# Which engine reads the small products of a four-layer network: from VectorE to ScalarE in layers 2 and 3

## The chip, the cores and the metric

The kernel runs on one core of a Trainium2 chip. The core has a matrix engine (TensorE, PE in the profile; its weight loads are PEld), VectorE (DVE), ScalarE (ACT), GpSimd (POOL) and SyncE (SP), which issues transfers. Each engine works through its own list of instructions, and semaphores tie the lists together. Matmul results land in a small accumulator memory, PSUM, and another engine has to read them out of it; in this kernel VectorE and ScalarE do that.

The metric is the time on the device in microseconds (us), the median of several executions. Before the change it is 2778.64 us, the median of 3 executions that lie between 2772.06 and 2782.84.

## What is computed

The input `x` is 4 images of 512 channels and 32x32 pixels (1024 tokens), in float32. Four layers follow one another. Each normalizes by groups (32 groups of 16 channels), computes something, and adds it to its input:

```python
x = x + L0(gn(x))   # attention, 8 heads, heads mixed before the softmax, instance norm of the probabilities
x = x + L1(gn(x))   # channel gate: mean over pixels -> 9-qubit circuit -> linear -> sigmoid, times gn(x)
x = x + L2(gn(x))   # attention, 8 heads, 1x1 convolutions for q, k, v and output
x = x + L3(gn(x))   # memory: the 8 best of 2048 items per token, softmax, weighted sum

def gn(v, G=32, eps=1e-5):
    g = v.reshape(B, G, C // G, H, W)
    m = mean(g, axis=(2, 3, 4)); s = var(g, axis=(2, 3, 4))
    return (g - m) / sqrt(s + eps)
```

Besides the large products there are thus many tiny ones. For each group norm the means and the deviations of 512 channels are averaged over groups of 16 channels, by a matmul with a constant 128x128 matrix. The gate of layer 1 needs two small matmuls for the circuit, one for its nine expectation values and one for the linear layer. Each of these yields at most 128x4 numbers.

## The kernel before

The kernel handles layers 0 and 1 image by image in a first loop and layers 2 and 3 in later loops. Work of the next or the last image that has to be fitted in between is written as Python generators: each `yield` ends a step, and the main loop takes a step or two between its large pieces. `pin` keeps an instruction in program order on its engine.

The group norm of all layers:

```python
def group_coeffs_parts(mean, var, tag):
    ...
    ps = small_ps(f"gps_{tag}")
    pin(nc.tensor.matmul(ps[:, 0:n], gavg, mean, start=True, stop=True))
    gm = tile_("gm")
    pin(nc.vector.tensor_copy(gm, ps[:, 0:n]))
    yield
    dm, sq = tile_("dm"), tile_("gsq")
    nc.gpsimd.tensor_sub(dm, mean, gm)
    nc.gpsimd.tensor_mul(sq, dm, dm)
    nc.gpsimd.tensor_add(sq, sq, var)
    yield
    ps2 = small_ps(f"gps2_{tag}")
    pin(nc.tensor.matmul(ps2[:, 0:n], gavg, sq, start=True, stop=True))
    ve = tile_("gve")
    pin(nc.vector.tensor_scalar_add(ve, ps2[:, 0:n], GN_EPS))
    yield
    rstd = tile_("grstd")
    rsqrt(rstd, ve)                      # on GpSimd
    yield gm, rstd, dm
```

The gate of layer 1 uses it with the tag `b`, layer 2 with `c`, layer 3 with `d`. After it the gate's generator, `gating(b)`, goes on in the same manner:

```python
    # twice, for the two layers of the circuit:
    ps = small_ps(f"amp_{b}_{l}"); products(ps)
    u = small.tile([P, KC], F32, tag="amp", ...)
    pin(nc.vector.tensor_copy(u, ps[:, 0:KC]))
    yield
    ...                                  # the last two qubits are rotated on GpSimd
    # expectation values
    ps = small_ps(f"z_{b}"); ...         # 8 matmuls of one column
    pin(nc.vector.tensor_copy(zr, ps[0:NQ, 0:2]))
    pin(nc.vector.reciprocal(zr[:, 1:2], zr[:, 1:2]))
    yield
    nc.gpsimd.tensor_mul(zr[:, 0:1], zr[:, 0:1], zr[:, 1:2])
    yield
    ps = small_ps(f"gate_{b}"); ...      # 4 matmuls of one column
    pin(nc.vector.tensor_copy(gate, ps[:, 0:KC]))
    yield
    nc.gpsimd.tensor_add(gate, gate, fcb)
    yield
    pin(nc.scalar.activation(gate, gate, AF.Exp, scale=-1.0))
    ...
```

At the border between layer 1 and layer 2 the PSUM pools are set up anew. From there a small product takes a buffer of the pool that holds the attention scores, which has three:

```python
stage.close()
pairs.clear()
stage = ctx.enter_context(ExitStack())
ps_s = stage.enter_context(tc.tile_pool(name="ps_s2", bufs=3, space=PSUM))
ps_m = stage.enter_context(tc.tile_pool(name="ps_m2", bufs=2, space=PSUM))

def small_ps(name):
    return ps_s.tile([P, 2 * NB], F32, tag="sc", name=name)
```

The main loop of layer 2 works in units. A unit is four blocks of 128 keys for two heads and 512 queries; 16 units make an image. While the scores of a unit are made, the values of the unit before it are summed:

```python
def scores2(b, u, before=None):
    def exp2():
        e = places2[:, count[0] % 6]; count[0] += 1
        nc.scalar.activation(e, scs[len(es)], AF.Exp); es.append(e)
    for i, t in enumerate(range(t0, t0 + 4)):
        sc = ps_s.tile([P, 2, NB], F32, tag="sc", ...)
        for r in range(2):
            pin(nc.tensor.matmul(sc[:, r, :], k block, q block, start=True, stop=True))
        scs.append(sc)
        if before is None or i < 2:
            exp2()
    if before is not None:
        apply2(b, before, exp2)          # 8 matmuls into pv; the last two exp2() in between
    ...                                  # sums of the exponentials: gpsimd.tensor_add, vector.tensor_add

def finish2(b):                          # every second unit, at the head of apply2
    rsp = ps_s.tile([P, 2, NB], F32, tag="sc", ...)[:, 0, :]
    ...                                  # two matmuls with ones: the row sums
    nc.scalar.copy(ri, rsp)
    nc.vector.reciprocal(ri, ri)
    nc.vector.tensor_mul(o, pv, ri)
    ...                                  # two gpsimd.dma_start of a row of ri

for b in range(B):
    behind = ...                         # norm3(b - 1), tag d; for b = 0 the gating of the last images
    ahead = ...                          # prepare2(b + 1), tag c
    for s, u in enumerate(UNITS2):
        ...
        if s >= 1: scores2(b, u, UNITS2[s - 1])
        for _ in range(2):
            if s >= 3: next(behind, None)
            if s >= 8: next(ahead, None)
```

So the small steps of `behind` and `ahead` stand between one unit and the scores of the next. (A float32 matmul shows as two in the profile, so the 8 of a unit's scores are 16 there.)

Of the kernel before, what the change touches and what calls it, by code (L numbers as in the profile page):

```python
# [20 lines left out]
KC = C // P  # L21
# [6 lines left out]
NQ = 9  # L28
# [4 lines left out]
GN_EPS = 1e-5  # L33
# [8 lines left out]
def fast_net(ctx: ExitStack, tc: tile.TileContext, a: dict, out: bass.AP, flag: bass.AP):  # L42
    nc = tc.nc
# [12 lines left out]
    def pin(ins):  # L56

        return tc.keep_in_program_order(ins)

    def small_ps(name):  # L60
        return pt_bank
# [60 lines left out]
    def rsqrt(dst, src):  # L122

        nc.gpsimd.tensor_tensor(
            dst, src, mhalf[:dst.shape[0], :dst.shape[1]], ALU.pow
        )


    def group_coeffs_parts(mean, var, tag):

        n = mean.shape[1]

        def tile_(name):
            return small.tile(
                [P, n], F32, tag=f"{name}{n}{tag[0]}", bufs=2, name=f"{name}_{tag}")

        ps = small_ps(f"gps_{tag}")
        pin(nc.tensor.matmul(ps[:, 0:n], gavg, mean, start=True, stop=True))  # L140
        gm = tile_("gm")
        pin(nc.vector.tensor_copy(gm, ps[:, 0:n]))
        yield
        dm, sq = tile_("dm"), tile_("gsq")
        nc.gpsimd.tensor_sub(dm, mean, gm)
# [3 lines that stand above are left out]
        ps2 = small_ps(f"gps2_{tag}")  # L149
        pin(nc.tensor.matmul(ps2[:, 0:n], gavg, sq, start=True, stop=True))  # L150
        ve = tile_("gve")
        pin(nc.vector.tensor_scalar_add(ve, ps2[:, 0:n], GN_EPS))
        yield
        rstd = tile_("grstd")
        rsqrt(rstd, ve)
        yield gm, rstd, dm

    def coeffs(mean, var, tag):

        found = None  # L160
        for found in group_coeffs_parts(mean, var, tag):
            if found is None:
                yield
        return found
# [109 lines left out]
    def first():  # L274
# [13 lines left out]
        def stats(k):  # L288
            mv = small.tile([P, 2], F32, tag="mv0", name=f"mv0_{k}")
            st = small.tile([P, 2, 6], F32, tag="bnst", name=f"st_a0_{k}")  # L290
            for i in range(2):
                pin(nc.vector.bn_stats(st[:, i, :], xn[:, k, i * NB:(i + 1) * NB]))
            pin(nc.vector.bn_aggr(mv, st.rearrange("p i s -> p (i s)")))
            parts[k] = group_coeffs_parts(mv[:, 0:1], mv[:, 1:2], f"a0_{k}")
# [490 lines left out]
    def gating(b):  # L785

        mv1 = img[b]["mv1"]
        gm, rstd, dm = yield from coeffs(mv1[:, 0, :], mv1[:, 1, :], f"b{b}")
        y = small.tile([P, KC], F32, tag="amp", name=f"amp_{b}")
        nc.gpsimd.tensor_mul(y, dm, rstd)  # L790
        yield

        def turned(l, products):
            ps = small_ps(f"amp_{b}_{l}")
            products(ps)
            u = small.tile([P, KC], F32, tag="amp", name=f"amp_{b}_{l}")
            pin(nc.vector.tensor_copy(u, ps[:, 0:KC]))
            yield
            us = small.tile([P, 2, KC], F32, tag="ampt", name=f"ampt_{b}_{l}")
            for i in range(2):  # L800
                for n in range(2):
                    a_ = sincos[:, n, l * NQ + i:l * NQ + i + 1]
                    nc.gpsimd.tensor_scalar_mul(us[:, n], u, a_)
                u_v, sin_v, cos_v = (t.rearrange("p (hi t lo) -> p hi t lo", t=2, lo=2 >> i)
                                     for t in (u, us[:, 0], us[:, 1]))
                nc.gpsimd.tensor_sub(u_v[:, :, 0], cos_v[:, :, 0], sin_v[:, :, 1])
                nc.gpsimd.tensor_add(u_v[:, :, 1], cos_v[:, :, 1], sin_v[:, :, 0])
            return u

        u = yield from turned(0, lambda ps: pin(nc.tensor.matmul(  # L810
            ps[:, 0:KC], turn[:, 0], y, start=True, stop=True)))
        yield

        def second(ps):
            pin(nc.tensor.matmul(ps[:, 0:KC:2], turn[:, 1], u[:, 0:KC:3], start=True, stop=True))
            pin(nc.tensor.matmul(ps[:, 1:KC:2], turn[:, 2], u[:, 1:3], start=True, stop=True))

        u = yield from turned(1, second)
        pr = small.tile([P, KC], F32, tag="amp", name=f"pr_{b}")
        nc.gpsimd.tensor_mul(pr, u, u)  # L820
        yield
        ps = small_ps(f"z_{b}")
        for i, m in enumerate((signs, None)):
            for k in range(KC):
                pin(nc.tensor.matmul(
                    ps[0:NQ, i:i + 1], ones[:, 0:NQ] if m is None else m[:, k, :],
                    pr[:, k:k + 1], start=(k == 0), stop=(k == KC - 1),
                ))
        zr = small.tile([NQ, 2], F32, tag="zr", name=f"zr_{b}")
        pin(nc.vector.tensor_copy(zr, ps[0:NQ, 0:2]))  # L830
        pin(nc.vector.reciprocal(zr[:, 1:2], zr[:, 1:2]))
        yield
        nc.gpsimd.tensor_mul(zr[:, 0:1], zr[:, 0:1], zr[:, 1:2])
        yield
        ps = small_ps(f"gate_{b}")
        for k in range(KC):
            pin(nc.tensor.matmul(
                ps[:, k:k + 1], fcw[:, k * P:(k + 1) * P], zr[:, 0:1], start=True, stop=True))
        gate = small.tile([P, KC], F32, tag="gate", name=f"gate_{b}")
        pin(nc.vector.tensor_copy(gate, ps[:, 0:KC]))  # L840
        yield
        nc.gpsimd.tensor_add(gate, gate, fcb)
        yield

        pin(nc.scalar.activation(gate, gate, AF.Exp, scale=-1.0))
        yield
        nc.gpsimd.tensor_scalar_add(gate, gate, 1.0)
        yield
        pin(nc.vector.reciprocal(gate, gate))
        yield  # L850
        s1 = const.tile([P, KC], F32, tag=f"s1_{b}", name=f"s1_{b}")
        t1 = const.tile([P, KC], F32, tag=f"t1_{b}", name=f"t1_{b}")
        nc.gpsimd.tensor_mul(s1, rstd, gate)
        nc.gpsimd.tensor_mul(t1, gm, s1)
        nc.gpsimd.tensor_scalar_mul(t1, t1, -1.0)
        nc.gpsimd.tensor_scalar_add(s1, s1, 1.0)
        mv2 = const.tile([P, 2, KC], F32, tag=f"mv2_{b}", name=f"mv2_{b}")
        nc.gpsimd.tensor_mul(mv2[:, 0, :], mv1[:, 0, :], s1)
        nc.gpsimd.tensor_add(mv2[:, 0, :], mv2[:, 0, :], t1)
        nc.gpsimd.tensor_mul(mv2[:, 1, :], mv1[:, 1, :], s1)  # L860
        nc.gpsimd.tensor_mul(mv2[:, 1, :], mv2[:, 1, :], s1)
        l2[b] = (mv2, s1, t1)
# [332 lines left out]
    def mid(b, s):  # L1195
        before = b - 1
        if s == TC - 1:
            state["sum_v"] = sum_v(b)
        if TC - 1 <= s <= TC:
            next(state["sum_v"])  # L1200
        if b > 0:
            if s == 3:
                state["norm"] = instance_norm(before)
            if 3 <= s < 7 or OUT - 2 <= s <= OUT:
                next(state["norm"], None)
            if OUT <= s + 1 < OUT + 16 and s % 2:
                image_piece(before, (s + 1 - OUT) // 4, (s + 1 - OUT) // 2 % 2)
            if OUT < s <= OUT + 16 and s % 2 == 0:
                piece_out(before, (s - 2 - OUT) // 4, (s - 2 - OUT) // 2 % 2)
            if s == NEXT:  # L1210
                state["behind"] = chain(state["behind"], gating(before))
        if NEXT - 3 <= s:
            next(state["ahead"])
        next(state["behind"], None)
# [41 lines left out]

    stage.close()
    pairs.clear()
    stage = ctx.enter_context(ExitStack())
    ps_s = stage.enter_context(tc.tile_pool(name="ps_s2", bufs=3, space=PSUM))  # L1260
    ps_m = stage.enter_context(tc.tile_pool(name="ps_m2", bufs=2, space=PSUM))
# [18 lines left out]
    for b in range(B):  # L1280
        last = b + 1 == B
        behind = chain(
            behind if b else state["behind"], norm3(b - 1) if b > 0 else gating(B - 1))
        ahead = prepare3(0) if last else prepare2(b + 1)
        for s, u in enumerate(UNITS2):
# [697 lines left out]
@with_exitstack  # L1983
def net_kernel(ctx: ExitStack, tc: tile.TileContext, a: dict, out: bass.AP):


    with tc.tile_pool(name="keep", bufs=1) as keep:
        flag = keep.tile([1, 1], mybir.dt.int32, tag="flag", name="flag")
        fast_net(tc, a, out, flag)
        again = tc.nc.values_load(flag, min_val=0, max_val=1)  # L1990
    with tc.If(again > 0):
        general_net(tc, a, out)
# [61 lines left out]
```

## Time and profile before

| | value |
|---|---|
| median of 3 executions | 2778.64 us (2772.06 to 2782.84) |
| span of the profiled execution | 2776.2 us |
| mean granted TensorE clock | 0.982 of full speed |
| first and last score matmul of layer 2 start | 1380.9 and 2250.0 us |
| 1375 to 2260 us: TensorE, VectorE, ScalarE, GpSimd busy | 847.3, 326.9, 304.4, 356.9 of 885 us |
| 2360 to 2460 us (in layer 3): TensorE, VectorE busy | 100.0, 80.5 of 100 us |
| duration of a small read on VectorE (128x4, from PSUM) | 0.15 us |

The page of the profile gives the busy time of each engine over the whole span, the span in 40 slices, and the costliest groups of instructions. Other views of the same trace are used too. The waits list, for each engine, which instruction sat idle until which other one had ended, with the total, the number and the longest. The timeline lists instructions in order of time, with consecutive ones of the same kind merged into a row (start, length, engine, line of the kernel, operation, output and inputs, and in brackets the idle time before it and what ended it). The table by stage gives busy time and granted clock in chosen stretches. In all of them an L with a number is a line of the kernel; the names `gps_`, `gm`, `gve`, `amp`, `z`, `zr` and `gate` are the small products and the tiles they are read into, `sc_c` the scores of layer 2, `pv_c` its sums of values, `rs_c` its row sums, and `eT` and `e` the buffers of its exponentials and their sums.

### The profile page before, as it was taken

How to read it: one execution, taken by the hardware profiler on the slowest of the kernel's cores; microseconds unless marked ns; L12 is line 12 of the kernel's file. 1: busy time of each engine (PE TensorE's matmuls, PEld its weight loads, DVE VectorE, ACT ScalarE, POOL GpSimd, SP SyncE). 2: the span in 40 equal slices, each digit the busy share in tenths (PEclk: the TensorE clock that was granted, in tenths of full speed). 3: DMA queues.
4: the chain of work that ended last, by engine and by line, in shares of the span. 5: the costliest groups of instructions: out<-in, count | busy, mean ns of one | idle time of the engine just before them, and what ended most of it. 6: DMA issues, size and time to landing. Idle time of an engine off the chain costs nothing.

```text
span 2776.2 us, 46960 instructions
## 1 busy us (share of the span) xinstructions
PE 2597.5 (94%) x18286; PEld 1178.0 (42%) x18286; DVE 1502.6 (54%) x2407; ACT 1005.8 (36%) x1128; POOL 1243.1 (45%) x1947
## 2 busy tenths in 40 slices
PE   7988998989989898989989999999999999999995
PEld 3443444545445444545433433343344334444442
DVE  4488347871578426872234224413523446888886
ACT  0466336551565426551144024214512532221210
POOL 2266415552456515553066026304601635666664
PEclk9999999999999999999999999999999999999997
DMA  2488537880687527784400030021002016766665
GB/s 77 107 209 203 139 87 212 219 216 30 165 217 207 157 80 196 194 216 175 142 3 1 31 121 1 16 73 64 1 31 91 1 35 189 217 185 215 184 185 149
DMA packets 159321, 349.82 MB, mean 126 GB/s; under 512 B 32361, under 2 KB 65129, under 8 KB 155378
## 3 DMA queue, kind: packets, MB, share of 16 engines
q1 hardware_dynamic: 86304, 167.04, 20.9%
q0 software_dynamic: 51200, 142.93, 19.1%
q10 hardware_dynamic: 21586, 36.76, 4.5%
q8 instruction: 147, 2.41, 0.4%
q14 instruction: 84, 0.69, 0.1%
HBM read 178.57 MB, written 33.69 MB: 76 GB/s over the span
## 4 chain that ended last, share of the span: by engine, by line
PE 75%; DMA 7%; ACT 6%; POOL 4%; DVE 4%; issue 2%; SPq 1%; ACTq 0%; POOLq 0%; DVEq 0%
PE at L1068 16%; PE sc L425 7%; PE mx L183 7%; PE sc_c L947 6%; PE pv L485 6%; PE pv_c L980 6%; DMA s<-ss 5%; PE pt L384 4%; ACT ss L431 4%; PE sc L183 4%; PE p L183 3%; PE v L195 3%; PE k L183 3%; PE q L183 3%; PE pt L658 3%
## 5 line engine op out<-in xcount | busy, mean ns | idle before, releaser
L458 DVE STREAM_TRANSPOSE eT<-e 128x1024 f32<-128x1024 f32 x256 | 317.4, 1242 | 275.5 <-ACT e L452 273.8
L438 POOL DMA_DIRECT2D s<-ss x512 | 259.7, 515 | 399.2 <-ACT ss L431 327.4
L1085 POOL DMA_INDIRECT got<-in_mem,ix x256 | 277.8, 1085 | 210.1 <-DVE tmx L1091 94.9
L941 ACT ACTIVATE eT<-sc_c 128x1024 f32<-128x1024 f32 x256 | 248.1, 1021 | 316.2 <-PE sc_c L947 232.8
L431 ACT COPY ss<-sc 128x1024 f32<-128x1024 f32 x256 | 258.9, 1011 | 260.3 <-PE sc L425 203.2
L474 DVE BATCH_NORM_STATS2 st<-e 128x6 f32<-128x256 f32 x1024 | 341.6, 405 | 0.0
L965 POOL TENSOR_TENSOR e<-eT 128x1024 f32<-128x1024 f32 x96 | 227.8, 2374 | 208.1 <-ACT eT L941 177.7
L425 PE MATMUL sc<-k,q 64*32 64x512 f32 x4096 | 287.6, 617 | 24.6 <-ACT ss L431 19.5
L452 ACT ACTIVATE e<-mx 128x1024 f32<-128x1024 f32 x256 | 262.5, 1028 | 69.9 <-PE mx L445 29.4
L966 DVE TENSOR_TENSOR eT<-eT,e 128x1024 f32<-128x1024 f32 x96 | 122.5, 1277 | 303.4 <-POOL e L965 303.4
L947 PE MATMUL sc_c<-q,k 64*128 64x512 f32 x1024 | 248.4, 618 | 37.7 <-ACT eT L941 9.8
L485 PE MATMUL pv<-eT,v 128*64 128x128 f32 x4096 | 256.9, 280 | 0.0
L485 PEld LDWEIGHTS pv<-eT,v 128*64 128x64 f32 x4096 | 226.7, 139 | 64.1 <-issue 62.5
L980 PE MATMUL pv_c<-eT,v 128*64 128x512 f32 x1024 | 234.5, 600 | 0.0
L445 PE MATMUL mx<-s,wmix 32*32 32x512 f32 x4096 | 159.4, 618 | 42.4 <-DMA s<-ss 40.6
L1109 DVE SCALAR_TENSOR_TENSOR acc<-got,et,acc 128x512 f32<-128x512 f32 x224 | 168.5, 752 | 8.0
L947 PEld LDWEIGHTS sc_c<-q,k 64*128 64x128 f32 x1024 | 93.2, 189 | 176.5 <-issue 74.6
L1007 DVE RECIPROCAL ri_c<-ri_c 128x512 f32<-128x512 f32 x32 | 107.0, 3345 | 96.1 <-ACT ri_c L1006 96.1
L1073 ACT COPY att<-at 128x1024 f32<-128x1024 f32 x64 | 64.8, 1012 | 217.1 <-PE at L1068 217.0
L961 POOL TENSOR_TENSOR eT<-eT 128x1024 f32<-128x1024 f32 x32 | 75.6, 2361 | 145.1 <-ACT eT L941 144.9
L561 POOL TENSOR_TENSOR o<-pv,rb 64x256 f32<-64x256 f32 x128 | 111.2, 868 | 64.6 <-ACT pv L548 57.6
L980 PEld LDWEIGHTS pv_c<-eT,v 128*64 128x64 f32 x1024 | 70.9, 138 | 156.1 <-issue 155.8
(314 smaller groups left out, 3293.2 us busy)
## 6 DMA issues: line engine op xcount, KB each, us to landing
s<-ss SPq DMA_DIRECT2D x512, 128.0 KB
s<-ss POOLq DMA_DIRECT2D x512, 128.0 KB, 4.5
rb<-r POOLq DMA_DIRECT2D x64, 128.0 KB, 5.8
o<-o SPq DMA_DIRECT2D x32, 256.0 KB
xr<-in_x ACTq DMA_DIRECT2D x32, 256.0 KB
x<-xr SPq DMA_DIRECT2D x32, 256.0 KB
xr_c<-x SPq DMA_DIRECT2D x32, 256.0 KB
x<-xr_c SPq DMA_DIRECT2D x32, 256.0 KB
```

What stands on the lines that cost most here:

```text
L183: pin(nc.tensor.matmul(ps[:, n, :], w[:, k, m * P:(m + 1) * P], rhs(k, n), start=(k == 0), stop=(k == KC - 1),))
L425: pin(nc.tensor.matmul(sc[m * NS:(m + 1) * NS, r, :], q[r * HD:(r + 1) * HD, m, s * NS:(s + 1) * NS], k_[r * HD:(r + 1) * HD, m, n * NB:(n ...
L431: pin(nc.scalar.copy(ss[:, :, n * NB:(n + 1) * NB], sc))
L438: pin(relays[r].dma_start(out=s2[r * KC + m::NH], in_=ss[m * NS:(m + 1) * NS, r, :]))
L452: pin(nc.scalar.activation(e[:, half].rearrange("p r qq k -> p (r qq k)"), flat2(pairs[f"mx{half}"]), AF.Exp))
L458: pin(nc.vector.transpose(eT[:, j % 2].rearrange("p b (qq i r) x -> p i r qq b x", qq=2, i=4)[:, i, 2 * half:2 * half + 2], e[:, half].rea ...
L474: pin(nc.vector.bn_stats(st[:, i, 2 * half + r, qq, :], e[:, half, r, qq, :]))
L485: pin(nc.tensor.matmul(pv[r * HD:(r + 1) * HD, gp, :], I["v"][:, t, g * HD:(g + 1) * HD], eT[:, j % 2, t, :, 4 * g:4 * g + 4], start=(t == ...
L947: pin(nc.tensor.matmul(sc[:, r, :], I["k"][r * HD:(r + 1) * HD, m, t * P:(t + 1) * P], I["q"][r * HD:(r + 1) * HD, m, n * NB:(n + 1) * NB] ...
L980: pin(nc.tensor.matmul(pv[r * HD:(r + 1) * HD, :], I["v"][:, t, h * HD:(h + 1) * HD], e[:, r, :], start=(t == 0), stop=(t == TC - 1),))
L1068: pin(nc.tensor.matmul(sc[:, n * NB:(n + 1) * NB], xn3[b][:, k, tt * P:(tt + 1) * P], memT[k][:, i0:i0 + NB], start=(k == 0), stop=(k == K ...
L1085: pin(nc.gpsimd.indirect_dma_start(out=got[:, i, :], out_offset=None, in_=a["mem"], in_offset=bass.IndirectOffsetOnAxis(ap=ix[:, i:i + 1], ...
```

## The change

From the border between layers 1 and 2 on, the small products are read out of PSUM by ScalarE in place of VectorE. It is meant to let a small product give back its buffer without standing in VectorE's list behind longer instructions. The deviations were read with the constant `GN_EPS` added in the same instruction; now ScalarE copies them, and GpSimd adds the constant in a further one. The reads on ScalarE are not pinned to program order. Layers 0 and 1 keep their reads, except for those gates that are still being worked on when layer 2 begins.

```diff
+    by_scalar = []
+
+    def take_small(dst, ps):
+
+        if by_scalar:
+            nc.scalar.copy(dst, ps)
+        else:
+            pin(nc.vector.tensor_copy(dst, ps))
...
         gm = tile_("gm")
-        pin(nc.vector.tensor_copy(gm, ps[:, 0:n]))
+        take_small(gm, ps[:, 0:n])
         yield
...
         ve = tile_("gve")
-        pin(nc.vector.tensor_scalar_add(ve, ps2[:, 0:n], GN_EPS))
+        if by_scalar:
+            nc.scalar.copy(ve, ps2[:, 0:n])
+            nc.gpsimd.tensor_scalar_add(ve, ve, GN_EPS)
+        else:
+            pin(nc.vector.tensor_scalar_add(ve, ps2[:, 0:n], GN_EPS))
         yield
...
             u = small.tile([P, KC], F32, tag="amp", name=f"amp_{b}_{l}")
-            pin(nc.vector.tensor_copy(u, ps[:, 0:KC]))
+            take_small(u, ps[:, 0:KC])
             yield
...
         zr = small.tile([NQ, 2], F32, tag="zr", name=f"zr_{b}")
-        pin(nc.vector.tensor_copy(zr, ps[0:NQ, 0:2]))
+        take_small(zr, ps[0:NQ, 0:2])
         pin(nc.vector.reciprocal(zr[:, 1:2], zr[:, 1:2]))
...
         gate = small.tile([P, KC], F32, tag="gate", name=f"gate_{b}")
-        pin(nc.vector.tensor_copy(gate, ps[:, 0:KC]))
+        take_small(gate, ps[:, 0:KC])
         yield
...
     stage.close()
     pairs.clear()
+    by_scalar.append(True)
     stage = ctx.enter_context(ExitStack())
```

## The prediction, made before the changed kernel was run

> **What bounds the kernel now.** I read the page first, for which engine fills the span; then who TensorE waits for in the stretch the change touches; then one such wait in the timeline; then the clock.
>
> Busy time and share of the span, from the page:
>
> ```profile
> PE 2597.5 (94%) x18286; PEld 1178.0 (42%) x18286; DVE 1502.6 (54%) x2407; ACT 1005.8 (36%) x1128; POOL 1243.1 (45%) x1947
> ```
>
> TensorE sets the time, and no other engine is over 54%. The change switches on when layer 2's loop begins, and layer 2 runs from 1381 us (first `sc_c` matmul) to about 2260. In 1375 to 2260 the table of busy time by stage gives TensorE 847.3 of 885 us: 37.7 us idle. The waits of TensorE in that window say for whom (waiter, released by: us in total, times, longest):
>
> ```profile
> PE sc_c L947 <- ACT eT L941: 9.8, 4, 4.8
> PE sc_c L947 <- DVE gm_d L142: 5.6, 3, 2.1
> PE sc_c L947 <- DVE amp L797: 4.6, 2, 2.9
> PE sc_c L947 <- DVE gve_c L152: 3.3, 2, 1.6
> PE sc_c L947 <- DVE gve_d L152: 3.1, 3, 1.0
> PE sc_c L947 <- DVE xr L624: 2.3, 1, 2.3
> PE sc_c L947 <- DVE gm_c L142: 2.2, 2, 1.1
> PE sc_c L947 <- DVE zr L830: 2.0, 1, 2.0
> PE sc_c L947 <- DVE gm_b L142: 1.8, 1, 1.8
> PE sc_c L947 <- DVE gate L840: 1.4, 2, 1.0
> PE sc_c L947 <- DVE gve_b L152: 1.0, 1, 1.0
> ```
>
> Without `xr` and `eT`, nine of these lines name a small product that VectorE reads: 5.6+4.6+3.3+3.1+2.2+2.0+1.8+1.4+1.0 = 25.0 us in 17 waits, two thirds of the idle time. All hit `sc_c`, the score tile, because small products and scores share three PSUM buffers: the product takes one, the next two score tiles take the others, and the third score tile needs the product's buffer back. (Where two products follow each other, the second score tile already does.) One wait in the timeline (start, us, engine, line, operation):
>
> ```profile
> 1669.37 3.34 DVE L1007 RECIPROCAL ri_c<-ri_c 128x512 f32<-128x512 f32 x1
> ...
> 1670.54 0.39 PE L140 MATMUL gps_d<-mv_d,gavg 128*128 128x4 f32 x2
> ...
> 1672.76 1.23 DVE L966 TENSOR_TENSOR eT<-eT,e 128x1024 f32<-128x1024 f32 x1
> ...
> 1673.90 0.68 DVE L1008 TENSOR_TENSOR eT<-pv_c,ri_c 128x512 f32<-128x512 f32 x1
> 1674.50 0.15 DVE L142 COPY gm_d<-gps_d 128x4 f32<-128x4 f32 x1
> ...
> 1674.71 1.99 PE L947 MATMUL sc_c<-q,k 64*128 64x512 f32 x8 [1.87 <-DVE gm_d L142]
> ```
>
> The product is finished at 1670.93. Its 0.15 us copy starts at 1674.50, because a 3.34 us reciprocal, an addition and a multiplication stand ahead of it on VectorE. TensorE starts two score tiles, then stands 1.87 us.
>
> The idle time is not the whole cost. An undisturbed set of four score tiles takes 3.63 us until the next operation starts (1689.99 in the chain; also 1705.21 to 1708.85). With `gm_d` it takes 1670.85 to 1676.62, 5.77: 2.14 more for 1.87 idle, since after the stall the two halves no longer overlap end to start (about 0.27 each). Two stalls cost much more, and the clock says why (stretch: us, TensorE busy, granted clock, DMA):
>
> ```profile
> 1466.00:1470.20 4.20, 4.20 (x14) 0.66 0.00 0
> 1478.50:1483.00 4.50, 4.47 (x12) 0.62 0.00 0
> ```
>
> They follow the 2.94 us wait for the second `amp` and the 2.01 us wait for `zr`. Twelve matmuls that should take 2.72 us (12 x 0.227) take 4.18 and 4.47.
>
> [...] the 0.15 us copy sat behind 5.25 us of work. [...] half-clock stretches follow these two stalls, [...] and the 2.12 us wait for the third `gm_d` (2163.13) shows none. [...] `ri_c` copies stand among exponentials with no gap of their own (0.59 us for 512 columns), and the 128x4 activation on `gate` takes 0.21 us.
>
> **The change part by part.** Set side by side, the instruction streams of the two kernels are the same on TensorE and on SyncE; VectorE loses 21 small reads, ScalarE gains 21, GpSimd gains 8 additions of the constant.
>
> 1. Removed from VectorE: 21 x 0.15 = 3.2 us. VectorE is busy 327 of 885 us here; this alone is worth nothing.
> 2. Added to ScalarE: 21 x about 0.21 = 4.4 us, an estimate from the `gate` activation. ScalarE is busy 304 of 885 us. In its order each copy stands after the fourth exponential of one unit and before the first of the next. In the example ScalarE is free from 1670.30 to 1672.09, so the copy would start just after 1670.93 and be done about 1671.2. The third score tile wants the buffer at about 1672.6 (1670.85 + 2 x 0.87). No stall is left. In the double cases the first buffer is wanted 0.87 us after the first score tile starts (1461.90 + 0.87 = 1462.77; the two `amp` products end about 1461.74, copy until about 1462.0): enough too.
> 3. Added to GpSimd: 8 x about 0.23 = 1.8 us (the 128x4 constant addition on `gate` is 0.23). GpSimd is busy 357 of 885 us. The addition lengthens the chain to the next small product, which lies a unit (7.2 us) later, and the chain starts about 3 us earlier. Hidden.
> 4. Taken off TensorE's path. I add, for each of the 17 stalls, the time from the first score tile to what follows the fourth, less 3.63:
>  - last image's gating: `gate` 1.26, `gm_b` 2.08, `gve_b` 1.31, first `amp` 1.93, second `amp` 4.62, `zr` 3.98, second `gate` 0.66: 15.8 us
>  - group norm before layer 3: `gm_d` 2.14, 1.93, 2.39 and `gve_d` 3 x 1.32: 10.4 us
>  - group norm before layer 2: `gm_c` 2 x 1.39, `gve_c` 2 x 1.92: 6.6 us
>
>  Sum 32.9 us: 25.0 idle, 17 x 0.27 = 4.6 of broken overlap, and 3.1 of half clock.
> 5. In layer 3 two reads move, `gm_d` and `gve_d` of the last image. TensorE has no idle stretch there (100.00 of 100 us from 2360 to 2460); the 3.5 and 2.0 us that VectorE waited for these products are slack. Worth 0.
>
> GpSimd's order also improves: the DMA issue that waits for the reciprocal now often stands behind the small chain rather than ahead of it.
>
> I keep 31.5 of 32.9: 2778.6 - 31.5 = 2747.
>
> **The rivals.**
> - *Another wait takes the place.* With the stalls gone, units in the gating stage run at TensorE's 7.2 to 8.1 us, and GpSimd, busy 78 of 135 us in 1375 to 1510, must keep up with rotations and sums. It frees the exponentials' buffers; ScalarE already waited 3.8 us for `amp` and 2.5 us for `e` there. For it: these waits lie exactly in this stage. Against it: 78 + 1 of the 119 us left is 67%, the waits followed late VectorE reads, and the next product of the chain has 2 to 3 us of margin by my count. If true, a third of the 15.8 us goes: 2752.
> - *ScalarE becomes late.* A copy that waits for its product holds up the exponentials behind it. Against it: the product always precedes those scores on TensorE, so the copy never waits longer than they do; and ScalarE is at 34%. If it cost 0.3 us in each of 17 places: 2752.
> - *The wait is a label and the real one is behind it.* The fourth score tile waits for the first exponential anyway. In undisturbed units 16 score matmuls run 3.63 us without a gap, so that wait is met in time. If it hid half of each stall: about 2762.
> - *More than the sum.* Only where fewer idle stretches also change the clock elsewhere (the half-clock stretch after the image start at 1391 follows an untouched wait). At most some 3 us: 2743.
>
> **Range and chances.** The three times before span 2772 to 2783, so the noise is about 5 us. The sum gives 2747, the likely rivals 2752, the worst 2762: I take 2739 to 2760. A gain over 2% would need 55.6 us, more than all the idle time of TensorE in layer 2 (37.7 us): chance 0.01. Slower by over 2% would need a new wait of over 3 us at each of 17 places: 0.01.
>
> **What would show it.** Right: no line of TensorE's waits in layer 2 names a small product; the image-start waits (`eT` 9.8, `xr` 2.3, `xr_c` 0.5) stay; the score stretches after a product take 3.6 us; the clock in the gating stage has no half stretch but the first; the copies on ScalarE take about 0.2 us within 0.5 us of their product; layer 2 is about 32 us shorter, layers 0, 1 and 3 unchanged. Wrong: `sc_c` waiting for ScalarE's `gm`, `gve` or `amp`, or for `eT`, by several us in all; small matmuls waiting for GpSimd; or a half clock that stays.

## The result and the profile after

The changed kernel takes 2751.86 us (median of 6 runs, 2747.59 to 2757.4); the kernel before took 2780.18 us beside it (6 runs). The ratio is 0.9901 (95% interval 0.9884 to 0.9918): 28.3 us less, 1.0%. Predicted were 31.5 us less, 2747.

Layer 2, from its first score product to its last row-sum product, went from 877.6 us (1380.87 to 2258.46 in the trace before) to 853.2 us (1378.20 to 2231.35): 24.4 us less. Layers 0 and 1, which the change does not touch, ended 2.7 us earlier. The start of layer 2 lies between 1373.7 and 1391.7 us in the traces of this study, so those 2.7 us are not put down to the change, and the length of layer 2 is a better gauge than the whole time.

The page of the changed kernel, busy time by engine:

```profile
PE 2588.1 (94%) x18286; PEld 1177.9 (43%) x18286; DVE 1520.4 (55%) x2386; ACT 1007.7 (37%) x1149; POOL 1264.0 (46%) x1955
```

VectorE has 21 instructions fewer, ScalarE 21 more, GpSimd 8 more, as counted. The waits of TensorE from layer 2 to the end (waiter, releaser: us in total, times, longest):

```profile
PE stp L1127 <- DVE acc L1122: 19.9, 2, 12.5
PE sc_c L960 <- ACT eT L954: 10.2, 4, 4.6
PE amp L828 <- POOL amp L820: 4.3, 1, 4.3
PE sc_c L960 <- DVE xr L637: 2.3, 1, 2.3
```

The nine lines that named a small product, 25.0 us in 17 waits, are gone. The image starts (`eT` 10.2, before 9.8) and `xr` are as they were, and so is the `stp` wait at the end of layer 3; the 0.5 us for `xr_c`, which were to stay, are gone too. One line is new: the product of the second half of a rotation waits 4.3 us for GpSimd. TensorE and GpSimd around it, from the timeline (start, us, engine, line, operation, in brackets idle time and releaser):

```profile
1448.89 0.57 POOL L816 TENSOR_SCALAR ampt<-amp,sincos 128x4 f32<-128x4 f32 x2
1454.39 1.10 POOL L1024 DMA_DIRECT2D fcw<-ri_c  x2 [4.93 <-issue]
1455.50 0.21 POOL L819 TENSOR_TENSOR amp<-ampt 128x2 f32<-128x2 f32 x1
1455.65 0.20 POOL L820 TENSOR_TENSOR amp<-ampt 128x2 f32<-128x2 f32 x1
```
```profile
1455.91 0.59 PE L828 MATMUL amp<-amp,turn 128*128 128x2 f32 x2 [4.30 <-POOL amp L820]
...
1457.29 6.14 PE L960 MATMUL sc_c<-q,k 64*128 64x512 f32 x16
```

A pair of row transfers (`fcw<-ri_c`, two rows of reciprocals that the kernel tests for their range at its end) stands on GpSimd between the two products of the second rotation and the two additions that finish it. GpSimd is free at 1449.46 and stands 4.93 us in front of it. TensorE needs the result at about 1451.6 and gets it at 1455.85. In the kernel before, the same pair stood ahead of the whole first rotation:

```profile
1456.71 1.13 POOL L1011 DMA_DIRECT2D fcw<-ri_c  x2 [3.06 <-issue]
1457.86 0.60 POOL L803 TENSOR_SCALAR ampt<-amp,sincos 128x4 f32<-128x4 f32 x2
```

In the changed kernel, after the wait, the score set takes 6.14 us and the small products 0.57 to 0.59 us, both longer than undisturbed (3.70 and 0.36 to 0.39 us). The table by stage shows why (stretch: us, busy of TensorE, weight loads, VectorE, ScalarE, GpSimd, granted clock, DMA share, GB/s):

```profile
1455.90:1463.40 7.50, 7.49 (x24) 3.80 (x24) 1.25 (x1) 2.38 (x4) 7.50 (x12) 0.58 0.00 0
1463.40:1470.00 6.60, 6.60 (x48) 2.75 (x48) 3.53 (x2) 3.01 (x6) 5.54 (x7) 1.00 0.01 2
```

In the slow stretch the score set's weight loads, taken two at a time, start every 0.85 us (1458.31, 1459.16, 1460.01), in the set at 1468.59 every 0.43 us: this is the half clock.

The wait and the half clock after it (score set 2.44 us over 3.63, the small products some 0.6) cost about 7.4 us: the gating stretch, from the first `gate` product to the second score set after the second `gate` product, went from 81.45 to 73.07 us, 8.4 less where 15.8 were to come. In the second image the stretch with both norms (from the score set before `gm_d` to the one after `gve_c`) went from 69.19 to 62.44, 6.75 less for the 6.77 that the prediction has for its four stalls.

### The profile page after: what moved, and what is told of

The parts are those of the page before. It is cut to its first block, busy times and chain, and to the rows that moved or that the text cites. A ratio compares the mean times of both kernels' runs of the same rounds, so it can differ in the third digit from the quotient of the medians.

```text
span 2749.0 us, 46995 instructions
## 1 busy us (share of the span) xinstructions
PE 2588.1 (94%) x18286; PEld 1177.9 (43%) x18286; DVE 1520.4 (55%) x2386; ACT 1007.7 (37%) x1149; POOL 1264.0 (46%) x1955
## 4 chain that ended last, share of the span: by engine, by line
PE 81%; DMA 7%; ACT 5%; DVE 3%; issue 1%; POOL 1%; SPq 1%; ACTq 0%; POOLq 0%; DVEq 0%
PE at L1081 16%; PE sc_c L960 8%; PE pv_c L993 8%; PE sc L438 7%; PE mx L196 7%; PE pv L498 6%; DMA s<-ss 4%; PE pt L397 4%; PE p L196 4%; PE sc L196 4%; ACT ss L444 4%; PE v L208 3%; PE k L196 3%; PE q L196 3%; PE pt L671 3%
## 5 line engine op out<-in xcount | busy, mean ns | idle before, releaser
L979 DVE TENSOR_TENSOR eT<-eT,e 128x1024 f32<-128x1024 f32 x96 | 132.9, 1384 | 276.0 <-POOL e L978 276.0
L960 PE MATMUL sc_c<-q,k 64*128 64x512 f32 x1024 | 244.3, 616 | 12.5 <-ACT eT L954 10.2
```

What stands on the lines that cost most here:

```text
L960: pin(nc.tensor.matmul(sc[:, r, :], I["k"][r * HD:(r + 1) * HD, m, t * P:(t + 1) * P], I["q"][r * HD:(r + 1) * HD, m, n * NB:(n + 1) * NB] ...
```

## The experiments

Every kernel was timed beside the kernel before on its own chip. "Layer 2" is its length in the profiled run, 877.6 before and 853.2 after. "Image starts" are the four waits of a score product for an exponential at the start of an image, and behind the plus sign what the half clock after them cost: a stretch's length times one less its granted clock, for the 7.5 us after each of these waits, and between the first score product and the first of them. Such stretches at the second and third image, first in the changed kernel, then in the one with rows by SyncE (columns as in the table by stage above):

```profile
1646.88:1654.38 7.50, 7.50 (x28) 2.42 (x30) 0.00 (x0) 2.96 (x4) 4.13 (x2) 0.79 0.00 1
1885.40:1892.90 7.50, 7.50 (x26) 2.39 (x28) 0.00 (x0) 2.80 (x3) 3.93 (x2) 0.77 0.01 2
```
```profile
1647.01:1654.51 7.50, 7.50 (x34) 2.80 (x36) 0.87 (x1) 4.42 (x5) 4.70 (x2) 1.00 0.00 1
1884.01:1891.51 7.50, 7.50 (x34) 2.80 (x36) 0.86 (x1) 4.41 (x5) 4.70 (x2) 1.00 0.01 2
```

These losses lie between 10.2 and 16.3 us, and their parts differ between two runs of one kernel too (10.0 + 2.9 and 8.4 + 5.1). So the last column but one takes them off: it is what layer 2 is shorter than before without image starts on either side.

| kernel | time, us | ratio to before (95%) | layer 2, us | image starts, us | layer 2 shorter without them, us | waits around small products, us |
|---|---|---|---|---|---|---|
| kernel before | 2780.18 | | 877.6 | 9.8 + 4.7 | | 25.0 |
| changed kernel | 2751.86 | 0.9901 (0.9884 to 0.9918) | 853.2 | 10.2 + 6.1 | 26.2 | 4.3 (rotation) |
| after, rows by SyncE | 2744.08 | 0.9891 (0.9858 to 0.9925) | 843.1 | 10.0 + 2.9 | 32.9 | 0.7 |
| the same again | 2742.75 | 0.9867 (0.9850 to 0.9883) | 844.0 | 8.4 + 5.1 | 32.6 | 0.8 |
| after, rows written later | 2753.08 | 0.9923 (0.9893 to 0.9953) | 848.1 | 8.3 + 3.4 | 26.7 | 3.9 (rotation) |
| after, first pair by SyncE | 2757.31 | 0.9930 (0.9910 to 0.9950) | 853.2 | 8.2 + 5.0 | 23.1 | 5.9 |
| after, norms only | 2757.08 | 0.9932 (0.9906 to 0.9957) | 854.8 | 7.3 + 3.4 | 19.0 | 10.1 |
| before, short reciprocal | 2784.3 | 1.0027 (1.0013 to 1.0040) | 882.1 | 8.2 + 3.2 | -7.6 | 28.1 |
| before, rows by SyncE | 2774.62 | 0.9988 (0.9976 to 1.0001) | 873.6 | 6.9 + 5.1 | 1.5 | 23.6 |
| before, additions late | 2746.40 | 0.9890 (0.9867 to 0.9912) | 843.9 | 9.6 + 3.3 | 32.1 | 0 |
| before, both | 2741.75 | 0.9866 (0.9847 to 0.9884) | 841.5 | 6.8 + 3.4 | 31.8 | 0 |

### Row transfers by SyncE (after)

```diff
-            nc.gpsimd.dma_start(out=seen[i:i + 1, :], in_=ri[r * HD:r * HD + 1])
+            nc.sync.dma_start(out=seen[i:i + 1, :], in_=ri[r * HD:r * HD + 1])
```

> The changed kernel, with the two row transfers of finish2 issued by SyncE instead of GpSimd. In the changed kernel TensorE waits 4.30 us for the second amp product's input, whose last two GpSimd instructions stand behind such a row transfer that waits for the reciprocal, and the half clock after it costs about 3.1 us more. Theory 1 (the waiting transfer ahead of the rotation on GpSimd): that wait goes and the clock stays whole, so 7 us less than the changed kernel, about 2745 against the 2751.9 measured, and no small product in TensorE's waits of layer 2. Theory 2 (GpSimd is simply too busy there, its small instructions stretched from 0.6 to 1.6 us a pair): the rotation still ends late, the wait shrinks by at most 1.1 us, and the time stays at about 2750.

Measured 2744.08 us, layer 2 843.1. The wait of the rotation is gone, and GpSimd goes through both halves without idle time (timeline of this kernel):

```profile
1455.07 1.46 POOL L816 TENSOR_SCALAR ampt<-amp,sincos 128x4 f32<-128x4 f32 x2
1456.62 0.19 POOL L819 TENSOR_TENSOR amp<-ampt 128x2 f32<-128x2 f32 x1
```
```profile
1458.55 0.38 PE L828 MATMUL amp<-amp,turn 128*128 128x2 f32 x2
...
1459.31 3.70 PE L960 MATMUL sc_c<-q,k 64*128 64x512 f32 x16
```

A wait of 0.7 us for `zr` at the `gate` product is new. Layer 2 is now 34.5 us shorter than before, and 32.9 without the image starts, as the sum had said. Of the 10.1 us between this layer 2 and the changed kernel's, 3.4 are image starts; the other 6.7 are the 7.4 us of the rotation's wait and its half clock less the new 0.7. So what the changed kernel lacked sat in this one wait. In whole time, the 7.8 us between the two medians were measured on two chips (by the ratios it is about 3 us, and 9 in the second run of this kernel); beside the version with rows written later, on the same chip, it is 9.0 us. In the kernel before and in the changed kernel a pair takes 0.96 to 1.14 us of GpSimd's time wherever it stands (the 64 rows 33.0 us in each); with SyncE issuing them, GpSimd's instructions have no row transfer left.

Not all of that gain is the wait. The time from the start of VectorE's last instruction (`flag`) to the end of the span fell from 13.14 to 9.17 us. It did so whenever the rows went to SyncE (13.23 to 9.15 in the kernel before, 13.01 to 8.92 with late additions). About 4 us of every SyncE version's gain therefore lie after the last computation. The trace puts them down to one instruction, the longest of three named `DRAIN` at the end of GpSimd's list (in the changed kernel, then in this one: ns least, median, most, first and last start):

```profile
L2064 POOLq DRAIN  x3: 46/107/7915, 2740.3 to 2748.8; - x3
```
```profile
L2064 POOLq DRAIN  x3: 40/107/3997, 2736.9 to 2741.5; - x3
```

It begins 4.3 to 4.4 us after `flag`, and some 0.8 us after its end the span ends, in both. With the 64 rows on GpSimd it takes 7.92 us (in the kernel before too), and 4.00 with none. That is about 0.06 us for each row, an estimate from 3.92 us over 64.

### The same rows, written later (after)

```diff
-            nc.gpsimd.dma_start(out=seen[i:i + 1, :], in_=ri[r * HD:r * HD + 1])
+            rows_due.append((i, ri[r * HD:r * HD + 1]))
...
     def finish2(b):
+        rows_out()          # nc.gpsimd.dma_start of what the block before left
```

> The changed kernel, with the two row transfers still issued by GpSimd, but each only when the next block of queries is finished, so that the reciprocal they read ended long ago and they wait for nothing. GpSimd has the same work as in the changed kernel, and one of the two transfers still stands inside the rotation. Theory 1 (it is the wait of the transfer, not its work): the 4.30 us wait goes, about 2745, equal to the version with SyncE. Theory 2 (GpSimd too busy): the wait stays over 3 us, about 2751. If this version stays at 2751 and the one with SyncE does not, it is the work of issuing and not the wait.

Measured 2753.08, with the wait still there. This edit failed to do what it was for. The transfers aren't pinned, and the scheduler put them back: in GpSimd's order the first of the pair reads the same `ri_c` as before and stands between the same two halves. In the timeline it still starts 3.23 us after that block's own reciprocal, which ends at 1454.25:

```profile
1450.91 3.34 DVE L1028 RECIPROCAL ri_c<-ri_c 128x512 f32<-128x512 f32 x1
```
```profile
1457.48 0.61 POOL L1006 DMA_DIRECT2D fcw<-ri_c  x1 [4.92 <-issue]
```

Its layer 2 is 5.1 us shorter than the changed kernel's, but 4.6 of that are image starts. It tells nothing on whether a later transfer would do. But the distance to the reciprocal gave the next question: nearly all other pairs for which GpSimd was free start 0.3 us after their reciprocal (0.28 to 0.30), and this one, the third of 32, in each kernel that had it 3.22 or 3.23 us after.

### The first pair alone by SyncE (after)

```diff
-            nc.gpsimd.dma_start(out=seen[i:i + 1, :], in_=ri[r * HD:r * HD + 1])
+            (nc.sync if b == 0 and due == (0, 0) else nc.gpsimd).dma_start(
+                out=seen[i:i + 1, :], in_=ri[r * HD:r * HD + 1])
```

> The changed kernel, in which only the very first pair of row transfers of layer 2 goes to SyncE; the pair that stands between the two halves of the rotation stays on GpSimd and becomes GpSimd's first and second pair less one. In every trace so far one pair, GpSimd's third, starts 3.22 us after its reciprocal ends, all the others 0.3 us after. Theory A (the extra 2.9 us belong to the third pair that GpSimd's queue issues, wherever it stands): it moves to the next pair, the wait of the second amp product shrinks from 4.3 us to under 2 us, and the time falls by 3 to 5 us to about 2748. Theory B (they belong to this place in the program): the pair still starts 3.2 us late, the wait stays at 4.3 us, 2752.

The mechanism came as theory A has it, the time didn't. The pair at the rotation starts 0.29 us after its reciprocal, and the extra 2.94 us have moved to the next pair, now GpSimd's third (its reciprocal ends at 1473.08). But that one stands between two steps of the next small chain, in front of the last instruction on `zr`, and the gate's product waits:

```profile
1454.40 1.10 POOL L1024 DMA_DIRECT2D fcw<-ri_c  x2 [1.99 <-DVE ri_c L1020]
1476.31 1.09 POOL L1024 DMA_DIRECT2D fcw<-ri_c  x2 [6.40 <-issue]
```
```profile
PE gate L850 <- POOL zr L846: 4.5, 1, 4.5
PE amp L828 <- POOL amp L820: 1.4, 1, 1.4
```

(First GpSimd's timeline, then TensorE's waits.) The time is 2757.31, where 2748 were expected, and layer 2 853.2: nothing gained. So of the 4.93 us, 2.0 are the wait for a reciprocal that had only begun, and 2.94 come with the third pair of the row transfers that GpSimd issues, at both places where it stood. Why the third, no view shows.

### The norms alone (after, with the gating's reads back on VectorE)

```diff
-        take_small(gm, ps[:, 0:n])
+        if tag[0] == "b":
+            pin(nc.vector.tensor_copy(gm, ps[:, 0:n]))
+        else:
+            take_small(gm, ps[:, 0:n])
```

The reads of `gve_b`, `amp`, `zr` and `gate` are put back in the same manner.

> The changed kernel, with the reads of the gating (gm and gve of tag b, amp, zr, gate) put back on VectorE; only those of tags c and d are on ScalarE. If the gains of the sites add up as the prediction sums them, tags c and d alone are worth 17.0 us: 2780.2 - 17.0 = 2763, and the gating part of the change only 8.4 of the predicted 15.8, since the changed kernel lies at 2751.9 with run-to-run noise of some 3 us. If the gains depended on one another, for instance if the freed VectorE helped the norms' units, it would lie at 2756 or below, or at 2770 or above.

Measured 2757.08, 6 us better than expected and between the two cases; 2.2 of the 6 us are the chip, on which the kernel before took 2778.01. Its waits hold the gating lines of the kernel before and none of the norms':

```profile
PE sc_c L963 <- DVE amp L813: 3.7, 2, 2.1
PE sc_c L963 <- DVE zr L846: 2.2, 1, 2.2
PE sc_c L963 <- DVE gm_b L152: 1.8, 1, 1.8
```

Layer 2 is 22.8 us shorter, 19.0 without the image starts, for the norms' 17.0. The `amp` waits are 0.9 us smaller here than before, and the longest of them is 2.1 and not 2.9. The clock stays whole after it, where before it was 0.66:

```profile
1466.16:1470.36 4.20, 4.20 (x20) 1.54 (x22) 0.00 (x0) 0.82 (x2) 3.78 (x12) 1.00 0.00 0
```

That spares another 1.4 us (4.20 times 0.34). With 17.0 + 0.9 + 1.4 = 19.3 for 19.0 the gains add up as the prediction has them.

### A short reciprocal (before)

```diff
-        nc.vector.reciprocal(ri, ri)
+        nc.vector.reciprocal(ri[:, 0:64], ri[:, 0:64])
```

It leaves out the reciprocals of 448 of 512 columns.

> The kernel before (reads on VectorE), with the reciprocal of layer 2 taken over 64 of its 512 columns, so that it lasts about 0.45 us instead of 3.34; the other columns stay without it, and the output is not that of the network. Theory 1, as the prediction put it (the small read is late because the reciprocal stands ahead of it): the stalls at the nine products that follow a reciprocal shrink by most of their 15.3 us idle, 2.4 of overlap and 1.7 of half clock: about 2762. Theory 2 (the read is late because an addition stands ahead of it that waits for GpSimd's sum, and the reciprocal lies in the shadow of that wait: in the example GpSimd's sum ends at 1672.73 and the addition starts at 1672.76): at most 2 us less, about 2779.

Measured 2784.3, slightly slower, and the waits are 28.1 us and not fewer. Taking 3 us out of VectorE's list in front of the small reads gained nothing. The reciprocal lay in time in which VectorE would have waited anyway, for the sum of two exponentials that GpSimd makes. In the kernel before, around the prediction's example:

```profile
1668.23 1.22 DVE L966 TENSOR_TENSOR eT<-eT,e 128x1024 f32<-128x1024 f32 x1 [2.54 <-POOL e L965]
1670.38 2.35 POOL L965 TENSOR_TENSOR e<-eT 128x1024 f32<-128x1024 f32 x1 [2.18 <-ACT eT L941]
```

GpSimd's sum ends at 1672.73, the reciprocal at 1672.71, and the addition that needs the sum starts at 1672.76. The addition, which stands in front of the small read, is what has to wait.

The edit did more than shorten the reciprocal, though. The row transfers now stand ahead of GpSimd's sum in the same place:

```profile
1665.04 1.00 POOL L1011 DMA_DIRECT2D fcw<-ri_c  x2 [2.02 <-DVE ri_c L1007]
1666.06 2.36 POOL L965 TENSOR_TENSOR e<-eT 128x1024 f32<-128x1024 f32 x1
```

So the sums come later, and with the third pair, which keeps GpSimd 4.95 us in front of a sum, the wait for the first `amp` grew from 1.65 to 4.81 us. This run alone would not clear the reciprocal; the times of the example do, and the late additions below.

### The row transfers by SyncE (before)

The same edit as above, in the kernel before.

> The kernel before, with its 64 row transfers of layer 2 issued by SyncE instead of GpSimd. This is the control for the same edit on the changed kernel, which brought 8 us there. Theory 1 (the transfer costs only where it stands between two halves of a rotation that TensorE waits for, and in the kernel before it stands in front of the rotation, in time that the stalls give away): the product of the second half does not wait today, so nothing is gained, 2778 within 2 us, and layer 2 stays at 876 to 880 us. Rival (issuing on GpSimd costs everywhere): about 8 us here too, 2770, layer 2 at 870 or under.

Measured 2774.62 us, 3.4 below the 2778 expected; the interval of the ratio, 0.9976 to 1.0001, includes no change. Layer 2 is 4.0 us shorter (a little outside the 876 to 880 expected), 1.5 without the image starts, and the end after `flag` is 4.1 shorter. The stalls stay (23.6 us for 25.0). So in the kernel before the transfers cost layer 2 between 1 and 2 us, most of it at the second `amp` (a wait of 1.74 us here, 2.94 before). The 6.4 to 6.7 us that they cost the changed kernel there (26.2 us shorter, against 32.6 and 32.9 with SyncE) lay for the most part hidden under the stalls that the change removed.

### The additions late (before; all reads stay on VectorE)

```diff
-            nc.vector.tensor_add(I["es", m, n], I["es", m, n], two)
+            late.append((I["es", m, n], two))
...
                 if s >= 8:
                     next(ahead, None)
+            sums_now()          # pinned nc.vector.tensor_add of what is in late
```

> The kernel before, with all small products still read by VectorE, but with VectorE's additions of the large sums written after the small reads, so that a small read no longer stands behind an addition that waits for GpSimd. Theory A (what made the read late was its place behind the addition, and any engine whose queue is free at that moment would do): the stalls where no reciprocal stands ahead disappear (gve_d, gve_b, gm_c, the second amp, gate2, about 13 us of the 25 us of idle time, with their clock losses about 18), the ones behind a reciprocal shrink by about 1 us each; about 22 us in all, 2756. Theory B (the read has to leave VectorE for ScalarE): under 5 us, 2773 to 2778. A point between the two would say that the reciprocal keeps the rest.

Measured 2746.40, layer 2 843.9: 33.7 us less (32.1 without the image starts), more than theory A asked for and far from theory B. (The profiled run of this kernel took 2756.75; its layer 2 began at 1391.7 us, 10.8 later than in the trace before, and the length of layer 2 is free of that.) Not one wait for a small product is left, also where a reciprocal stands ahead (TensorE's waits in layer 2, complete):

```profile
PE sc_c L954 <- ACT eT L948: 9.6, 4, 4.6
PE sc_c L954 <- DVE xr L624: 2.3, 1, 2.3
PE rs_c L1008 <- DVE eT L933: 1.0, 1, 1.0
PE sc_c L954 <- DVE xr_c L1032: 0.2, 1, 0.2
```

VectorE at the same product as in the prediction's example:

```profile
1661.62 3.35 DVE L1014 RECIPROCAL ri_c<-ri_c 128x512 f32<-128x512 f32 x1 [2.15 <-ACT ri_c L1013]
1665.08 0.69 DVE L1015 TENSOR_TENSOR eT<-pv_c,ri_c 128x512 f32<-128x512 f32 x1
1665.69 0.15 DVE L142 COPY gm_d<-gps_d 128x4 f32<-128x4 f32 x1
1665.76 3.17 DVE L933 TENSOR_TENSOR eT<-eT,e 128x1024 f32<-128x1024 f32 x2
```

The product starts at 1664.32 here, and the copy 1.37 us later; in the kernel before it was 3.96 us later (1670.54 and 1674.50). Two additions did that. One stood ahead of the reciprocal, which began 3.27 us after the start of its row-sum product (1666.10 to 1669.37) and here begins 1.74 us after (1659.88 to 1661.62). The other stood between reciprocal and multiplication. This is why the waits behind a reciprocal went too, and why the expected 22 us were too few: the reciprocal was late for the same reason as the read.

The read need not leave VectorE, then. Of the 5.25 us of work behind which the prediction found the copy, the expensive part was the addition of 1.23 us, which waits for another engine, and not the longest instruction, the reciprocal of 3.34 us.

### Both cheap edits, and the best version so far beside it

> The kernel before with both cheap edits: VectorE's additions of the sums written after the small reads (all reads stay on VectorE, nothing is added), and the row transfers issued by SyncE. By the waits of the first edit alone only 9.6 us at the starts of the images and about 1 us elsewhere are left in layer 2, and none of them hangs on GpSimd. If everything that small reads cost is already gone, the transfers bring nothing more: 2745 within 3 us, layer 2 at 842 to 844 us. Rival (transfers on GpSimd still cost several us there): 2740 or under, layer 2 at 838 or under.

> The changed kernel with its row transfers on SyncE once more, beside the version above on the same chip, to say which of the two ways is the shorter. Both have lost all small waits, so both should stand within 3 us of each other, at 2744 to 2746; if ScalarE as the reader has something of its own (its operations are off VectorE and start at once), this one is 3 us or more the shorter.

Measured on one chip: 2741.75 us for the kernel before with late additions and rows by SyncE, 2742.75 us for the changed kernel with rows by SyncE. The two can't be told apart (ratios 0.9866 and 0.9867). Layer 2 is 841.5 and 844.0 us; without the image starts both are about 32 us shorter than before (31.8 and 32.6). Against late additions alone, layer 2 is 2.4 us shorter, of which 2.7 are the image starts; the rest of the gain is the 4.1 us after `flag`. So the first of the two expectations holds inside layer 2 (nothing more from the transfers), and ScalarE as the reader has nothing of its own to give. Both versions are the fastest of the study; the one with late additions has on each computing engine as many instructions as the kernel before, less the 64 transfers of GpSimd.

## Why the prediction was right, and where it was not

- **The sum (step 4), right.** 32.9 us were added up over 17 stalls (the three parts named beside it make 32.7, by rounding). In the four versions without the stalls and with at most 1.0 us of new waits layer 2 is shorter by 34.5, 33.6, 33.7 and 36.1 us, and without the image starts by 32.9, 32.6, 32.1 and 31.8. The extra terms of broken overlap and half clock were needed: idle time alone would have given 25.0.
- **Which rival came: the wait that takes the place.** It was put at 2752 and 2751.86 was measured, but that closeness is luck: it took about 7.4 of the 15.8 us of the gating, a half rather than a third, and the six runs of the changed kernel lie between 2747.59 and 2757.4. It was argued against with "the next product of the chain has 2 to 3 us of margin by my count". The count left out the transfer in GpSimd's list. Its margin was exceeded by 4.3 us.
- **The failed step: "GpSimd's order also improves".** It was said that the DMA issue now often stands behind the small chain. At the one place that mattered it stands in the middle of it. It cost TensorE 4.30 us of wait and about 3.1 of half clock. In the kernel before, this pair stood ahead of the whole first rotation, where it made the second `amp` wait only 1.20 us longer (2.94, and 1.74 with rows by SyncE). The order of the lists was known before the run; which chain a transfer cuts was not asked.
- **The cause of the late read, half right.** It was given as a reciprocal, an addition and a multiplication that stand ahead. The late additions show that the additions are it: with them gone the reciprocal still stands ahead of the read, and no wait is left. The length of the reciprocal is not it, by the times of the example and by the short reciprocal, which gained nothing.
- **ScalarE (step 2), right.** The copies in layer 2 take 0.15 to 0.16 us (estimate 0.21) and follow at once; the `gve_b` product at 1435.6 is read at 1436.02. No score product waits for one.
- **GpSimd's eight additions (step 3), hidden, but mis-sized.** 0.23 us each was said; four of the eight take 1.25 to 1.32 us (below). No TensorE wait follows from them by itself.
- **Layer 3 (step 5), right.** From the last row sum to the end the traces have 517.7 us before and after.
- **The checks listed.** Score sets after a small product take 3.63 to 3.65 us until the next operation, except the one after the new wait; the half stretch that stays in the gating stage comes from that wait too. "Layer 2 about 32 us shorter" failed by 7.6 us, of which 1.8 are image starts.

## What to carry to other kernels

When a small read makes the pacing engine wait, look at what the reading engine itself waits for just ahead of it: writing that waiting instruction after the read (no work moved, none added) brought all that moving the read to another engine brought. Before counting on a removed stall, go through the lists of the other engines along the chain that is now next, and see what of another chain stands in the middle of it, DMA issues above all. Compare such edits by the length of the stage in the trace, since the stages around it moved by more than the edit was worth, and inside the stage take off waits that the edits do not touch, with the half clock that follows them: here these moved by up to 6 us.

## What the runs showed of the hardware

The eight new additions on GpSimd (128x4, one input) fall into two kinds (instructions of their line in the changed kernel: ns least, median, most):

```profile
L163 POOL TENSOR_SCALAR gve_d<-gve_d x4: 216/226/1249, 1670.9 to 2319.2; 128x4 f32<-128x4 f32 x4
L163 POOL TENSOR_SCALAR gve_c<-gve_c x3: 225/1319/1324, 1469.9 to 1948.7; 128x4 f32<-128x4 f32 x3
L163 POOL TENSOR_SCALAR gve_b<-gve_b x1: 1254/1254/1254, 1439.6 to 1439.6; 128x4 f32<-128x4 f32 x1
```
```profile
1439.51 1.22 DVE L979 TENSOR_TENSOR eT<-eT,e 128x1024 f32<-128x1024 f32 x1 [7.43 <-POOL e L978]
1439.56 1.25 POOL L163 TENSOR_SCALAR gve_b<-gve_b 128x4 f32<-128x4 f32 x1
```

The long one ends 0.08 us after the VectorE addition that began beside it, and so do the other three long ones, to 0.01 us, with the additions that they overlap. Of the short ones, one ran beside the reciprocal of `ri_c` (1469.88, 0.23 us) and one with no VectorE addition near it (2319.16, 0.22 us). But the other two short ones, which began 0.05 and 0.06 us ahead of such an addition, took 0.22 and 0.23 us all the same.

The granted clock was 0.58 in the 7.5 us after the 4.30 us wait and 1.00 in the rest of the gating (1411 to 1451 and 1463.4 to 1500), in line with the 0.66 and 0.62 that followed the 2.94 and 2.01 us waits of the kernel before, and the 0.59 after its 4.81 us wait at the image start (1391.0 to 1398.5). Between 2 and 3 us the length of a wait did not tell whether a half clock would follow: it did after 2.01 us (kernel before, `zr`, 0.62) and 2.37 us (changed kernel, third image, 0.77), and did not after 2.12 us (kernel before, third `gm_d`, 1.00 from 2163 to 2171), 2.31 us (rows by SyncE, third image, 1.00) and 2.50 us (norms only, third image, 1.00 in the 7.5 us after 1892.61).

Three things stay open: what holds four of GpSimd's eight additions for 1.25 to 1.32 us, why the third pair of GpSimd's row transfers takes 2.94 us longer than the others, and why the `DRAIN` at the end of GpSimd's list takes 3.92 us longer when GpSimd has issued the 64 rows.
